# Attention scores of a four-layer block from six bfloat16 products instead of nine, on 64-row halves of TensorE

## The chip, the cores and the metric

The kernel runs on one core of one Trainium2 chip, in one launch. The metric is device time in microseconds (us): 1566.85 us before, the median of three runs (1562.56, 1566.85, 1570.48). The profile shows one further execution with a span of 1563.8 us from its first to its last instruction.

The names of the engines in what follows: PE is TensorE (matmuls), PEld its weight loads, DVE is VectorE, ACT is ScalarE, POOL is GpSimd, SP is SyncE, which here only issues DMAs (SPq in the profile).

## What is computed

An input of 4 sequences of 1024 tokens of 128 features goes through four layers, each added to its input after a normalisation: an RWKV-like time and channel mixing, a mixture of 16 experts, a linear attention with decaying states, and softmax attention followed by a mixture of 8 experts. The change is in the softmax attention of the last layer:

```python
def _gqa(x, wq, wk, wv, wo):                       # 16 heads of 8 features, 4 key heads
    B, S, C = x.shape                              # 4, 1024, 128
    q = (x @ wq.T).reshape(B, S, 16, 8)
    k = (x @ wk.T).reshape(B, S, 4, 8)
    v = (x @ wv.T).reshape(B, S, 4, 8)
    k, v = jnp.repeat(k, 4, axis=2), jnp.repeat(v, 4, axis=2)
    attn = jnp.einsum('bqhd,bkhd->bhqk', q, k) / sqrt(8)
    attn = jnp.where(causal, attn, -inf)
    attn = jax.nn.softmax(attn, axis=-1)
    out = jnp.einsum('bhqk,bkhd->bqhd', attn, v).reshape(B, S, C)
    return out @ wo.T
```

All of it is float32 in the reference. A head has only 8 features, so that a score is a sum over 8 rows of TensorE's 128.

## The kernel before

**The stages.** Up to about 295 us the first layer runs, and the second begins. Up to about 660 us the second layer's experts run beside the linear attention of the first two sequences. From about 660 us on, the softmax attention of all four sequences runs, together with what is left of the linear attention (sequences 2 and 3, generator `stage_c`), the projections `heads`, and the last experts (generator `experts`). This last part stands under `tc.manual_schedule()`: its order is written out by the Python loops and nothing moves it. What stands before it is put into an order by the framework's scheduler.

**Scores from parts.** A float32 matmul of 512 columns keeps PE 0.86 us from start to start in the profile (two instructions), a bfloat16 one 0.22 us. `heads` splits queries and keys into three bfloat16 parts each (`parts3`) and stores them to HBM (`dq`, `dk`, with eight rows d to a part). `spread(b, h)` reads them back for a chunk of 512 tokens, so that nine products (part i of the query with part j of the key) stand under each other as rows of one bfloat16 matmul: 9 products of 8 features are 72 rows (`KROWS`). It issues 18 DMAs on SP, two for each product: one into `keys_r` (L950, 8 rows of 4 key groups), one into `queries_r` (L954, 8 rows of all 16 heads). Rows 125 to 127 (`MROWS` on) hold the row maximum of a query in three parts, against -1 in the keys, so that the score arrives with its maximum subtracted. Rows 72 to 124 are zeros in the queries, set once at the start with memsets on POOL (L868, L869) and two broadcast DMAs for each pair of tiles (L871, L874).

**Two passes over the scores.** For each sequence b and block i of 128 queries:

- `maxima(b, i)` computes scores with the queries as weights and takes row maxima on DVE. `late` treats the keys of the block's own 512-chunk: one matmul a head (L977), as many heads to a PSUM bank as fit (four, two, one, one, for 128, 256, 384, 512 keys), then one matmul of the 128x128 identity with the causal mask `later` that adds -1e30 on the last 128 keys of each head (L981), then a `tensor_reduce` (L985). `early` treats the first 512 keys for blocks 4 to 7, a head at a time: one matmul (L989), one reduce (L990). There are 352 `late` and 256 `early` units in all. Three banks (`to_max`) hold their results. `rows` splits the 16 maxima into three parts on POOL (L999 to L1002); PE turns them (L1005), DVE copies them (L1009), and three DMAs on SP place them into `queries_r` (L1013).
- `weighted(b, i)` computes the scores again with the keys as weights, 128 keys by 4 heads of 128 queries (`unit(j, g)`, L1049, 576 in all; g is one of the 4 key groups, j the key block). ACT takes the exponential (L1054); on the diagonal POOL zeroes what the mask hides (L1058). Two banks (`scores`) hold these. After eight units, four are multiplied with the values (`products`, L1041): four float32 matmuls, each on its own 32 columns of the array, into one bank.

**The order.** The main loop (L1323 to L1347) lets one `unit` of `weighted` run, then as many units of `maxima` of later blocks as the table `COURSE` asks for. Each is a tick; a tick also calls what is due (`later_on`), advances a `spread` by one step (`moving`), and now and then takes a step of `front()` (linear attention and heads of the next sequence) or of `behind_it` (experts of finished chunks). So sc (L1049), sm (L977, L981, L989), av (L1041) and the float32 matmuls of the other stages follow each other on PE in an order that is fixed.

**Weights.** `by_d` (L1397) orders the columns of wq and wk by feature first, so that the rows of `dq` and `dk` come out as `spread` reads them.

Of the kernel before, what the change touches and what calls it, by code (L numbers as in the profile page):

```python
# [12 lines left out]
BF = mybir.dt.bfloat16  # L13
# [5 lines left out]
P = 128  # L19
NB = 4  # L20
T = 1024
CH = 512
NH = T // CH
# [11 lines left out]
def r3(ap, a):  # L35
    return ap.rearrange("p (a b) -> p a b", a=a)
# [3 lines left out]
def sandwich(ctx: ExitStack, tc: tile.TileContext, x, vecs, cmats, rope, wa, wb, wc, wd, out):  # L40
# [3 lines left out]
    nc = tc.nc  # L44
# [718 lines left out]
    while running or behind_a or coming_a:  # L763
        if coming_a and count >= BEHIND:
            b, h = coming_a[0]
# [5 lines left out]
        for item in list(running):  # L771
            kind, b, h, steps = item
# [70 lines left out]
    pk = ctx.enter_context(tc.tile_pool(name="pk", bufs=1, side="left", reuse_waits="tile"))  # L843
    pe = ctx.enter_context(tc.tile_pool(name="pe", bufs=2, side="left", reuse_waits="tile"))
# [3 lines left out]
    nc.sync.dma_start(out=wdt, in_=wd[:, 0:328])  # L848
    identb = pk.tile([P, P], BF, name="identb")
    nc.gpsimd.tensor_copy(identb, ident)  # L850
    later = pk.tile([P, 4, P], BF, name="later")
    m = pe.tile([P, P], FP, tag="a", name="m", bufs=1)
    make_causal_mask(nc, m, MASKED)
    for k in range(4):
        nc.gpsimd.tensor_copy(later[:, k, :], m)
    wv_d, wo_d, wgate_d = wdt[:, 160:192], wdt[:, 192:320], wdt[:, 320:328]
    restart8 = restarts(4, 8, pk, "restart8")
    QSCALE = float(1.0 / np.sqrt(8).astype(np.float32))
# [1 line left out]

    KROWS, MROWS, ROWS = 72, P - 3, P
    keys_r = [pk.tile([P, NH, 4, CH], BF, name=f"keys_r{i}") for i in range(2)]
    queries_r = [pe.tile([P, 16, CH], BF, tag=f"qr{i}", name=f"queries_r{i}", bufs=1) for i in range(NH)]
    for kr, qr in zip(keys_r, queries_r):

        nc.gpsimd.memset(kr[64:128, 0, 0, :], -1.0)  # L868
        nc.gpsimd.memset(qr[64:128, 0, :], 0.0)  # L869
        first, others = qr[64:128, 0:1, :], qr[64:128, 1:16, :]  # L870
        nc.sync.dma_start(out=others, in_=first.to_broadcast([64, 15, CH]))  # L871
        kf = kr.rearrange("p a b t -> p (a b) t")
        first, others = kf[64:128, 0:1, :], kf[64:128, 1 : NH * 4, :]
        nc.sync.dma_start(out=others, in_=first.to_broadcast([64, NH * 4 - 1, CH]))  # L874

    def parts3(dst, src):

# [8 lines left out]
    moved = set()  # L886
# [55 lines left out]
    def spread(b, h):  # L942

        dq, dk = drams[b]
        kr = keys_r[b % 2]
        qr = queries_r[h]
        for i in range(3):
            for j in range(3):
                rows = slice(3 * i + j, KROWS, 9)
                nc.sync.dma_start(  # L950
                    out=kr[rows, h].rearrange("r g t -> r (g t)"),
                    in_=dk[h, j].rearrange("(d g) t -> d (g t)", d=8),
                )
                nc.sync.dma_start(  # L954
                    out=qr[rows].rearrange("r h t -> r (h t)"),
                    in_=dq[h, i].rearrange("(d h) t -> d (h t)", d=8),
                )
                if (i, j) == (2, 2):
                    moved.add((b, h))
                yield  # L960

    def maxima(b, i):


        qr, kr = queries_r[i // 4], keys_r[b % 2]
        tb = slice(i % 4 * P, (i % 4 + 1) * P)
        half = i // 4
        n_s = (i % 4 + 1) * P
        in_bank = CH // n_s
        ms = pe.tile([P, 2, 16], FP, tag="ms", name="ms", bufs=3)  # L970

        def late(h0):
            sc = to_max([P, CH], "sm")
            view = r3(sc[:, : in_bank * n_s], in_bank)
            for k in range(in_bank):
                h = h0 + k
                nc.tensor.matmul(  # L977
                    view[:, k, :], lhsT=qr[0:MROWS, h, tb], rhs=kr[0:MROWS, half, h // 4, 0:n_s],
                    start=(k == 0), stop=False, skip_group_check=True,
                )  # L980
            nc.tensor.matmul(  # L981
                view[:, :, n_s - P :], lhsT=identb, rhs=later[:, :in_bank, :], start=False, stop=True,
                skip_group_check=True,
            )
            nc.vector.tensor_reduce(ms[:, 0, h0 : h0 + in_bank], view, AX.X, ALU.max)  # L985

        def early(h):
            sc = to_max([P, CH], "sm")
            nc.tensor.matmul(sc, lhsT=qr[0:MROWS, h, tb], rhs=kr[0:MROWS, 0, h // 4, :], start=True, stop=True)  # L989
            nc.vector.tensor_reduce(ms[:, 1, h : h + 1], sc, AX.X, ALU.max)  # L990

        def rows():
            mp = pe.tile([P, 3, 16], BF, tag="mp", name="mp", bufs=3)
            left = pe.tile([P, 16], FP, tag="ml", name="ml", bufs=3)
            top = ms[:, 0]
            if half:
                top = pe.tile([P, 16], FP, tag="top", name="top_ms", bufs=3)
                nc.vector.tensor_reduce(top, ms.rearrange("p a h -> p h a"), AX.X, ALU.max)
            nc.gpsimd.tensor_copy(mp[:, 0], top)  # L999
            nc.gpsimd.tensor_sub(left, top, mp[:, 0])  # L1000
            nc.gpsimd.tensor_copy(mp[:, 1], left)
            nc.gpsimd.tensor_sub(mp[:, 2], left, mp[:, 1])  # L1002
            def turned():
                pm = to_max([48, P], "m_ps", BF)
                nc.tensor.transpose(pm, mp.rearrange("p i h -> p (i h)"), identb)  # L1005

                def kept():
                    mt = pe.tile([48, P], BF, tag="mt", name="mt", bufs=3)
                    nc.vector.tensor_copy(mt, pm)  # L1009

                    def placed():
                        for k in range(3):
                            nc.sync.dma_start(  # L1013
                                out=qr[MROWS + k : MROWS + k + 1, :, tb], in_=mt[16 * k : 16 * k + 16, :]
                            )
                        placed_rows.add((b, i))

                    later_on(3, placed)

                later_on(1, kept)  # L1020

            later_on(9, turned)

        units = [lambda h0=h0: late(h0) for h0 in range(0, 16, in_bank)]
        if half:
            units += [lambda h=h: early(h) for h in range(16)]
        return units + [rows]

    def weighted(b, i):


        qr, kr, va = queries_r[i // 4], keys_r[b % 2], vas[b]
        tb = slice(i % 4 * P, (i % 4 + 1) * P)

        def products():

            for _ in range(4):
                j, g, pr = held.popleft()[1:]
                if (j, g) == (0, 0):
                    pavs[b, i] = pp([P, CH], "av")  # L1040
                nc.tensor.matmul(  # L1041
                    pavs[b, i][32 * g : 32 * g + 32, :], lhsT=va[:, j, g, :], rhs=pr, start=(j == 0), stop=(j == i),
                )
            if j == i:
                later_on(1, finish)

        def unit(j, g):
            sc = scores([P, CH], "sc")
            nc.tensor.matmul(  # L1049
                sc, lhsT=kr[0:ROWS, j // 4, g, j % 4 * P : (j % 4 + 1) * P], rhs=qr[0:ROWS, 4 * g : 4 * g + 4, tb],  # L1050
                start=True, stop=True,
            )
            pr = pd.tile([P, CH], FP, tag="pr", name="pr", bufs=10)
            nc.scalar.activation(pr, sc, AF.Exp)  # L1054
            if j == i:

                every = r3(pr, 4)
                nc.gpsimd.affine_select(  # L1058
                    out=every, in_=every, compare_op=ALU.is_ge, fill=0.0, base=0,
                    pattern=[[0, 4], [1, P]], channel_multiplier=-1,  # L1060
                )
            held.append((products, j, g, pr))
            if len(held) > 7:
                held[0][0]()

        def finish():
            av = pd.tile([P, CH], FP, tag="avs", name="av_sb")
            nc.scalar.copy(av, pavs.pop((b, i)))
            if i % 4 == 0:
                sums[b, i // 4] = dram.tile([4, 4, 9, CH], FP, tag="sums", name="sums")  # L1070
            to = sums[b, i // 4].rearrange("g r d t -> g d r t")

            def stored():
                for g in range(4):
                    nc.sync.dma_start(out=to[g][:, :, tb], in_=r3(av[32 * g : 32 * g + 9, :], 4))
                if i % 4 == 3:
# [238 lines left out]
    with tc.manual_schedule():  # L1315
# [7 lines left out]
        for b, i in blocks:  # L1323
# [9 lines left out]
            w = 2 * i * (i + 1)  # L1333
# [36 lines left out]
def _arrays(i):  # L1370
# [25 lines left out]
    wc = [a[L1 + "Wq"], a[L1 + "Wk"], a[L1 + "Wv"], wo_rows, a[L1 + "Wbeta"]]  # L1396
    def by_d(w):  # L1397

        return w.reshape(P, -1, 8).transpose(0, 2, 1).reshape(P, -1)

    wd = [
        by_d(a[F1 + "wq"].T), by_d(a[F1 + "wk"].T), a[F1 + "wv"].T, a[F1 + "wo"].T, a[F1 + "gate_w"].T,
# [24 lines left out]
```

## Time and profile before

| What | Value |
|---|---|
| median of three runs | 1566.85 us |
| profiled execution, span | 1563.8 us |
| DVE busy in it | 1066.1 us |
| ACT busy in it | 845.7 us |
| POOL busy in it | 827.9 us |
| mean granted TensorE clock, as a share of full speed | 0.902 |
| L1049, matmuls sc | 576, 226.1 us busy |
| L977, matmuls sm of `late` | 512, 129.5 us busy |
| L981, mask matmuls of `late` | 352, 88.1 us busy |
| L989, matmuls sm of `early` | 256, 98.1 us busy |
| L1041, matmuls av | 1152 instructions (two for each float32 matmul), 174.9 us busy |
| L1054, exponentials on ACT | 576, 328.2 us busy |
| L985 and L990, maxima on DVE | 608, 213.1 and 166.2 us busy |
| DMAs of `spread` | 72 into `queries_r` of 128 KB, 72 into `keys_r` of 32 KB |
| DMAs that place maxima | 96 of 4 KB |

Matmuls are pipelined: a matmul's own time in the profile includes its way through the array, and the next may start before it ends. So the distance from start to start says what a matmul costs PE, not its duration. The view of chains follows the work back from the last instruction: to what released it, or to the instruction before it on its engine. The view of windows gives the busy time of each engine in a stretch, with the granted clock behind it.

### The profile page before, as it was taken

How to read it: one execution, taken by the hardware profiler on the slowest of the kernel's cores; microseconds unless marked ns; L12 is line 12 of the kernel's file. 1: busy time of each engine (PE TensorE's matmuls, PEld its weight loads, DVE VectorE, ACT ScalarE, POOL GpSimd, SP SyncE). 2: the span in 40 equal slices, each digit the busy share in tenths (PEclk: the TensorE clock that was granted, in tenths of full speed). 3: DMA queues.
4: the chain of work that ended last, by engine and by line, in shares of the span. 5: the costliest groups of instructions: out<-in, count | busy, mean ns of one | idle time of the engine just before them, and what ended most of it. 6: DMA issues, size and time to landing. Idle time of an engine off the chain costs nothing. (4 is left out here: it accounts for less than half of the span.)

```text
span 1563.8 us, 15069 instructions
## 1 busy us (share of the span) xinstructions
PE 1220.8 (78%) x4532; PEld 445.2 (28%) x4532; DVE 1066.1 (68%) x1755; ACT 845.7 (54%) x1565; POOL 827.9 (53%) x901
## 2 busy tenths in 40 slices
PE   4478788868687697877688698779876889889864
PEld 2123333313222232333133223223222333233211
DVE  5886965587757757668976986796379776477501
ACT  3668676536445454545345466534653474655541
POOL 5664575576838857752733655553355554223312
PEclk9779999969888899999889999978897999999986
DMA  3000101452222323101113122211130113111101
GB/s 113 14 7 0 46 29 40 104 117 86 87 60 85 94 68 105 55 19 60 45 53 91 37 58 92 63 53 57 36 98 23 58 43 101 51 55 44 57 24 61
DMA packets 62337, 93.35 MB, mean 60 GB/s; under 512 B 10097, under 2 KB 29809, under 8 KB 61553
## 3 DMA queue, kind: packets, MB, share of 16 engines
q1 hardware_dynamic: 53040, 75.63, 16.8%
q10 hardware_dynamic: 9216, 16.78, 3.3%
q8 instruction: 35, 0.57, 0.2%
q14 instruction: 46, 0.37, 0.1%
HBM read 76.38 MB, written 12.71 MB: 57 GB/s over the span
## 5 line engine op out<-in xcount | busy, mean ns | idle before, releaser
L1054 ACT ACTIVATE pr<-sc 128x512 f32<-128x512 f32 x576 | 328.2, 596 | 298.7 <-PE sc L1049 293.3
L985 DVE TENSOR_REDUCE ms<-sm 128x1 f32<-128x512 f32 (+3 forms) x352 | 213.1, 633 | 120.4 <-PE sm L981 113.7
L1049 PE MATMUL sc<-queries_r,keys_r 128*128 128x512 bf16 x576 | 226.1, 400 | 28.9 <-ACT pr L1054 26.2
L990 DVE TENSOR_REDUCE ms<-sm 128x1 f32<-128x512 f32 x256 | 166.2, 682 | 49.9 <-PE sm L989 49.6
L1041 PE MATMUL av<-pr,va 128*32 128x512 f32 x1152 | 174.9, 660 | 3.7 <-POOL pr L1058 3.7
L1058 POOL TENSOR_SCALAR_AFFINE_SELECT pr<-pr 128x512 f32<-128x512 f32 x128 | 95.2, 758 | 128.8 <-ACT pr L1054 126.8
L977 PE MATMUL sm<-keys_r,queries_r 125*128 125x512 bf16 (+3 forms) x512 | 129.5, 309 | 36.2 <-DVE ms L985 30.5
L1168 POOL TENSOR_TENSOR share<-n,every 128x512 f32<-128x512 f32 x64 | 81.5, 1291 | 84.7 <-DMA every<-row 65.0
L138 PE MATMUL ln_v<-rs,cm 128*128 128x512 f32 x176 | 106.4, 698 | 22.2 <-ACT rs L126 14.7
L989 PE MATMUL sm<-keys_r,queries_r 125*128 125x512 bf16 x256 | 98.1, 405 | 30.4 <-DVE ms L990 25.5
L633 POOL TENSOR_TENSOR kv<-vrep,phi 128x512 f32<-128x512 f32 x64 | 89.0, 1392 | 53.7 <-issue 25.9
L649 POOL TENSOR_TENSOR qs<-st,st 128x512 f32<-128x512 f32 x72 | 102.7, 1428 | 26.5 <-DVE st L639 18.7
L486 POOL TENSOR_TENSOR g<-g,x 128x512 f32<-128x512 f32 x72 | 95.5, 1328 | 30.6 <-ACT g L476 17.9
L478 POOL TENSOR_TENSOR x<-x,gate 128x512 f32<-128x512 f32 x64 | 84.0, 1314 | 36.9 <-ACT g L474 35.7
L1049 PEld LDWEIGHTS <-keys_r 128*128 128x128 bf16 x576 | 57.5, 102 | 137.6 <-issue 111.3
L138 PE MATMUL g_ps<-n,wbt 128*128 128x512 f32 x144 | 81.6, 658 | 18.2 <-DVE n L392 7.5
L465 PE MATMUL y_ps<-g,wbt 128*128 128x512 f32 x144 | 78.3, 629 | 18.1 <-DVE g L496 18.0
L981 PE MATMUL sm<-later,identb 128*128 128x128 bf16 (+2 forms) x352 | 88.1, 250 | 0.0
L138 PE MATMUL u_ps<-n,wbt 128*128 128x512 f32 x144 | 79.4, 634 | 9.8 <-DVE g L496 6.4
L496 DVE TENSOR_TENSOR g<-u_ps,g 128x512 f32<-128x512 f32 x72 | 49.5, 687 | 51.0 <-POOL g L486 31.7
L977 PEld LDWEIGHTS <-queries_r 125*128 125x128 bf16 x512 | 47.6, 100 | 104.1 <-issue 87.6
L1180 PE MATMUL y<-share,wexp 128*128 128x512 f32 x128 | 68.1, 621 | 5.2 <-POOL share L1168 5.0
(302 smaller groups left out, 2311.3 us busy)
## 6 DMA issues: line engine op xcount, KB each, us to landing
gate<-rows ACTq DMA_DIRECT2D x64, 256.0 KB
vrep<-v_rows SPq DMA_DIRECT2D x64, 256.0 KB
every<-row SPq DMA_DIRECT2D x64, 256.0 KB
queries_r<-dq SPq DMA_DIRECT2D x72, 128.0 KB
turn<-in_rope_dram SPq DMA_DIRECT2D x16, 256.0 KB
dq<-qp SPq DMA_DIRECT2D x8, 384.0 KB
keys_r<-dk SPq DMA_DIRECT2D x72, 32.0 KB
sums<-av_sb SPq DMA_DIRECT2D x128, 18.0 KB
```

The source lines that it names most:

```text
L138: nc.tensor.matmul(ps, lhsT=lhsT, rhs=rhs, start=True, stop=True)
L486: nc.gpsimd.tensor_mul(g, g, x)
L633: nc.gpsimd.tensor_mul(kvs[e], values.pop(e), k)
L649: nc.gpsimd.tensor_add(sums_e[e][0], s0, s1)
L977: nc.tensor.matmul(view[:, k, :], lhsT=qr[0:MROWS, h, tb], rhs=kr[0:MROWS, half, h // 4, 0:n_s], start=(k == 0), stop=False, skip_group_ch ...
L985: nc.vector.tensor_reduce(ms[:, 0, h0 : h0 + in_bank], view, AX.X, ALU.max)
L989: nc.tensor.matmul(sc, lhsT=qr[0:MROWS, h, tb], rhs=kr[0:MROWS, 0, h // 4, :], start=True, stop=True)
L990: nc.vector.tensor_reduce(ms[:, 1, h : h + 1], sc, AX.X, ALU.max)
L1041: nc.tensor.matmul(pavs[b, i][32 * g : 32 * g + 32, :], lhsT=va[:, j, g, :], rhs=pr, start=(j == 0), stop=(j == i),)
L1049: nc.tensor.matmul(sc, lhsT=kr[0:ROWS, j // 4, g, j % 4 * P : (j % 4 + 1) * P], rhs=qr[0:ROWS, 4 * g : 4 * g + 4, tb], start=True, stop=True,)
L1054: nc.scalar.activation(pr, sc, AF.Exp)
L1058: nc.gpsimd.affine_select(out=every, in_=every, compare_op=ALU.is_ge, fill=0.0, base=0, pattern=[[0, 4], [1, P]], channel_multiplier=-1,)
```

## The change

Six products are kept of nine: parts (0,0), (0,1), (1,0), (1,1), (0,2) and (2,0). With 8 features these are 48 rows, and three rows for the maximum make 51, which fit into 64. So two sets of rows lie in one tile: partitions 0 to 63 hold key groups 0 and 2 and heads 0 to 7 as the tiles count them, partitions 64 to 127 the other eight heads. `by_d` reorders the weights, so that the d-rows of a part come as 16 rows, for the two halves. In each half, row 8d+n holds product n of feature d; the maxima lie in slot 6 of features 0 to 2, and slot 7 is zero in the queries.

- `late`, `early` and `unit` read 64 partitions, of the one or the other half. Units take the halves in turn: g % 2 in `weighted`, n in `maxima`. The program puts these matmuls on 64x128 tiles of the array, at row 0 or row 64.
- The mask's identity would need 128 rows, so it is split: keys 0 to 63 of a block (`upper`, 128 columns a head) and keys 64 to 127 (`lower`, 64 columns a head), two matmuls of 64 rows for each `late` unit. Both are kept in both halves (`id_part`, `upper`, `lower`: 20 copies on POOL instead of 4).
- The maxima's rows are read in `maxima` too now, so that they must be zero by then: `spread` of the sequences after the first begins with a DMA that copies slot 7 onto slot 6.
- `spread` issues 12 DMAs (13 with that copy) in place of 18, of 16 partitions each, in 6 steps in place of 9; the placing of maxima 2 in place of 3, of 24 rows of 128 each.
- The tiles `keys_r` and `queries_r` are half as large. They are filled at the start by memsets of 128 partitions, and by eight broadcast DMAs into slots 6 and 7 alone, in place of four into 64 partitions.

```diff
-    later = pk.tile([P, 4, P], BF, name="later")
     m = pe.tile([P, P], FP, tag="a", name="m", bufs=1)
     make_causal_mask(nc, m, MASKED)
-    for k in range(4):
-        nc.gpsimd.tensor_copy(later[:, k, :], m)
+    HALF = P // 2
+    id_part = pk.tile([P, 2, P], BF, name="id_part")
+    upper = pk.tile([P, 4, P], BF, name="upper")
+    lower = pk.tile([P, 4, HALF], BF, name="lower")
+    for to in (slice(0, HALF), slice(HALF, P)):
+        for n in range(2):
+            nc.gpsimd.tensor_copy(id_part[to, n, :], identb[n * HALF : (n + 1) * HALF, :])
+        for k in range(4):
+            nc.gpsimd.tensor_copy(upper[to, k, :], m[0:HALF, :])
+            nc.gpsimd.tensor_copy(lower[to, k, :], m[HALF:P, HALF:])
...
-    KROWS, MROWS, ROWS = 72, P - 3, P
-    keys_r = [pk.tile([P, NH, 4, CH], BF, name=f"keys_r{i}") for i in range(2)]
-    queries_r = [pe.tile([P, 16, CH], BF, tag=f"qr{i}", name=f"queries_r{i}", bufs=1) for i in range(NH)]
...
+    PAIRS = [(0, 0), (0, 1), (1, 0), (1, 1), (0, 2), (2, 0)]
+    SLOTS, TOP = 8, 6
+    keys_r = [pk.tile([P, NH, 2, CH], BF, name=f"keys_r{i}") for i in range(2)]
+    queries_r = [pe.tile([P, 8, CH], BF, tag=f"qr{i}", name=f"queries_r{i}", bufs=1) for i in range(NH)]
+    for t, val in [(kr.rearrange("p a b t -> p (a b) t"), -1.0) for kr in keys_r] + [(qr, 0.0) for qr in queries_r]:
+
+        n = t.shape[1]
+        nc.gpsimd.memset(t[:, 0, :], val)
+        for slot in (TOP, TOP + 1):
+            first, others = t[slot::SLOTS, 0:1, :], t[slot::SLOTS, 1:n, :]
+            nc.sync.dma_start(out=others, in_=first.to_broadcast([P // SLOTS, n - 1, CH]))
...
@@ spread
-        for i in range(3):
-            for j in range(3):
-                rows = slice(3 * i + j, KROWS, 9)
...
+        if b:
+            nc.sync.dma_start(out=qr[TOP::SLOTS], in_=qr[TOP + 1 :: SLOTS])
+        for n, (i, j) in enumerate(PAIRS):
+            rows = slice(n, P, SLOTS)
+            nc.sync.dma_start(
+                out=kr[rows, h].rearrange("r g t -> r (g t)"),
+                in_=dk[h, j].rearrange("(d g) t -> d (g t)", g=2),
+            )
+            nc.sync.dma_start(
+                out=qr[rows].rearrange("r h t -> r (h t)"),
+                in_=dq[h, i].rearrange("(d h) t -> d (h t)", h=8),
+            )
...
@@ maxima
         def late(h0):
+            rows, first = half_of(h0 // 8), h0 % 8
...
-                    view[:, k, :], lhsT=qr[0:MROWS, h, tb], rhs=kr[0:MROWS, half, h // 4, 0:n_s],
+                    view[:, k, :], lhsT=qr[rows, h, tb], rhs=kr[rows, half, h // 4, 0:n_s],
...
-                view[:, :, n_s - P :], lhsT=identb, rhs=later[:, :in_bank, :], start=False, stop=True,
+                view[:, :, n_s - P :], lhsT=id_part[rows, 0, :], rhs=upper[rows, :in_bank, :], start=False, stop=False,
+                skip_group_check=True,
+            )
+            nc.tensor.matmul(
+                view[:, :, n_s - HALF :], lhsT=id_part[rows, 1, :], rhs=lower[rows, :in_bank, :], start=False, stop=True,
...
-            nc.tensor.matmul(sc, lhsT=qr[0:MROWS, h, tb], rhs=kr[0:MROWS, 0, h // 4, :], start=True, stop=True)
+            nc.tensor.matmul(
+                sc, lhsT=qr[rows, h % 8, tb], rhs=kr[rows, 0, h % 8 // 4, :], start=True, stop=True
+            )
...
-                        for k in range(3):
+                        for n in range(2):
+                            first = n * HALF + TOP
                             nc.sync.dma_start(
-                                out=qr[MROWS + k : MROWS + k + 1, :, tb], in_=mt[16 * k : 16 * k + 16, :]
+                                out=qr[first : first + 3 * SLOTS : SLOTS, :, tb], in_=mt[24 * n : 24 * n + 24, :]
                             )
...
-        units = [lambda h0=h0: late(h0) for h0 in range(0, 16, in_bank)]
+        units = [lambda h=h0 + 8 * n: late(h) for h0 in range(0, 8, in_bank) for n in range(2)]
         if half:
-            units += [lambda h=h: early(h) for h in range(16)]
+            units += [lambda h=h + 8 * n: early(h) for h in range(8) for n in range(2)]
...
@@ weighted
+            rows, of = half_of(g % 2), g // 2
...
-                sc, lhsT=kr[0:ROWS, j // 4, g, j % 4 * P : (j % 4 + 1) * P], rhs=qr[0:ROWS, 4 * g : 4 * g + 4, tb],
+                sc, lhsT=kr[rows, j // 4, of, j % 4 * P : (j % 4 + 1) * P], rhs=qr[rows, 4 * of : 4 * of + 4, tb],
...
@@ by_d
-        return w.reshape(P, -1, 8).transpose(0, 2, 1).reshape(P, -1)
+        return w.reshape(P, 2, 2, -1, 8).transpose(0, 2, 4, 1, 3).reshape(P, -1)
```

More of the change, by code (lines that the diff above doesn't have):

```diff
@@ L858, in sandwich, with half_of @@
     QSCALE = float(1.0 / np.sqrt(8).astype(np.float32))
-    KROWS, MROWS, ROWS = 72, P - 3, P
-    keys_r = [pk.tile([P, NH, 4, CH], BF, name=f"keys_r{i}") for i in range(2)]
-    queries_r = [pe.tile([P, 16, CH], BF, tag=f"qr{i}", name=f"queries_r{i}", bufs=1) for i in range(NH)]
[L866 to L874, printed above, removed]
+    PAIRS = [(0, 0), (0, 1), (1, 0), (1, 1), (0, 2), (2, 0)]
[8 more added lines that the diff above has]
+            nc.sync.dma_start(out=others, in_=first.to_broadcast([P // SLOTS, n - 1, CH]))
+    def half_of(half):
+        return slice(half * HALF, (half + 1) * HALF)
     def parts3(dst, src):
@@ L946, in spread @@
         qr = queries_r[h]
-        for i in range(3):
-            for j in range(3):
-                rows = slice(3 * i + j, KROWS, 9)
[L950 to L960, printed above, removed]
+        if b:
[10 more added lines that the diff above has]
+            )
+            if n + 1 == len(PAIRS):
+                moved.add((b, h))
+            yield
     def maxima(b, i):
@@ L975, in late @@
             for k in range(in_bank):
-                h = h0 + k
+                h = first + k
                 nc.tensor.matmul(
-                    view[:, k, :], lhsT=qr[0:MROWS, h, tb], rhs=kr[0:MROWS, half, h // 4, 0:n_s],
+                    view[:, k, :], lhsT=qr[rows, h, tb], rhs=kr[rows, half, h // 4, 0:n_s],
                     start=(k == 0), stop=False, skip_group_check=True,
@@ L987, in early @@
         def early(h):
+            rows = half_of(h // 8)
             sc = to_max([P, CH], "sm")
-            nc.tensor.matmul(sc, lhsT=qr[0:MROWS, h, tb], rhs=kr[0:MROWS, 0, h // 4, :], start=True, stop=True)
+            nc.tensor.matmul(
+                sc, lhsT=qr[rows, h % 8, tb], rhs=kr[rows, 0, h % 8 // 4, :], start=True, stop=True
+            )
             nc.vector.tensor_reduce(ms[:, 1, h : h + 1], sc, AX.X, ALU.max)
         def rows():
-            mp = pe.tile([P, 3, 16], BF, tag="mp", name="mp", bufs=3)
+            mp = pe.tile([P, 2, 3, 8], BF, tag="mp", name="mp", bufs=3)
             left = pe.tile([P, 16], FP, tag="ml", name="ml", bufs=3)
@@ L998, in rows @@
                 nc.vector.tensor_reduce(top, ms.rearrange("p a h -> p h a"), AX.X, ALU.max)
[L999 to L1002, printed above, removed]
+            top, left = r3(top, 2), r3(left, 2)
+            nc.gpsimd.tensor_copy(mp[:, :, 0], top)
+            nc.gpsimd.tensor_sub(left, top, mp[:, :, 0])
+            nc.gpsimd.tensor_copy(mp[:, :, 1], left)
+            nc.gpsimd.tensor_sub(mp[:, :, 2], left, mp[:, :, 1])
             def turned():
                 pm = to_max([48, P], "m_ps", BF)
-                nc.tensor.transpose(pm, mp.rearrange("p i h -> p (i h)"), identb)
+                nc.tensor.transpose(pm, mp.rearrange("p a i h -> p (a i h)"), identb)
                 def kept():
```

## The prediction

> **What bounds the kernel now.** I read the page first: busy shares, then the chain that ended last.
>
> ```profile
> PE 1220.8 (78%) x4532; PEld 445.2 (28%) x4532; DVE 1066.1 (68%) x1755; ACT 845.7 (54%) x1565; POOL 827.9 (53%) x901
> PE 19%; DVE 7%; ACT 4%; POOL 2%; issue 2%; SPq 2%; DMA 2%; POOLq 0%; ACTq 0%; DVEq 0%
> ```
>
> The chain covers 38% of the span only, its last 600 us; there PE holds half of it (19 of 38). The change lives in the stage from 660 us on, so I looked at that by windows of 50 us (busy time of PE, PEld, DVE, ACT, POOL, granted clock, DMA share, GB/s):
>
> ```profile
> 1000.00:1050.00 50.00, 33.27 (x142) 10.47 (x140) 46.75 (x59) 20.24 (x48) 32.36 (x26) 0.83 0.20 61
> 1150.00:1200.00 50.00, 33.62 (x153) 10.79 (x151) 44.05 (x60) 22.08 (x40) 28.88 (x25) 0.89 0.27 79
> 1300.00:1350.00 50.00, 47.06 (x262) 17.64 (x261) 25.91 (x47) 29.36 (x53) 16.82 (x29) 0.99 0.20 61
> 1450.00:1500.00 50.00, 43.43 (x217) 13.54 (x216) 17.29 (x44) 31.63 (x59) 14.53 (x19) 1.00 0.14 46
> ```
>
> Two regimes: where linear attention runs beside, DVE is full and PE has slack (33 of 50); where it doesn't, PE is full (47 of 50) and DVE and ACT are half idle. So what the change does to PE's own column of work counts for about half. The queue of exponentials confirms who is late: ACT waits 293.3 us for sc (L1049) in all.
>
> Then PE's timeline, start to start, in a full stretch:
>
> ```profile
> 1301.55 0.38 PE L989 MATMUL sm<-keys_r,queries_r 125*128 125x512 bf16 x1
> 1301.77 0.38 PE L1049 MATMUL sc<-queries_r,keys_r 128*128 128x512 bf16 x1
> 1302.08 1.07 PE L1041 MATMUL av<-pr,va 128*32 128x512 f32 x8
> 1303.08 0.39 PE L989 MATMUL sm<-keys_r,queries_r 125*128 125x512 bf16 x1
> ...
> 1308.87 1.02 PE L1180 MATMUL y<-share,wexp 128*128 128x512 f32 x2
> 1309.73 0.38 PE L1049 MATMUL sc<-queries_r,keys_r 128*128 128x512 bf16 x1
> ...
> 1359.33 0.22 PE L981 MATMUL sm<-later,identb 128*128 128x128 bf16 x1
> 1359.39 0.38 PE L1049 MATMUL sc<-queries_r,keys_r 128*128 128x512 bf16 x1
> ```
>
> Three prices come from it. A bfloat16 matmul of 512 columns costs 0.22 us (1301.55 to 1301.77), a mask of 128 columns 0.06. Going to the 32-column tiles of av costs 0.09 (sc to av is 0.31, not 0.22). Eight av instructions take 1.00 us where two instructions of that length on the full array take 0.86 (y to sc): four tiles of columns run side by side, and the way back costs some 0.10, once 0.04 for their staggered starts are off. Between float32 and bfloat16 on the full array nothing is lost (the 0.86).
>
> **The change, part by part.** I compared the two programs' instruction order: from the first score on, PE's matmuls follow each other as before, but for the added masks. The parts then:
>
> 1. Changes of tiling. Scores leave the full array for 64-row tiles, the float32 matmuls between them stay. Counted in the order: 377 changes of tile shape before, 679 after, so 302 more, each way between scores and float32. No row shows a change of rows; the nearest are the changes of columns, 0.09 and 0.10. In the timeline 263 of these 302 neighbours follow back to back, without a wait that could hide it. 263 x 0.10 = +26 us. Bounds: nothing, if rows change free of charge, to 302 x 0.10 = +30. I take +26.
>
> 2. Masks. 352 more matmuls, of 64 columns for each head in the bank: 256 units with one head, 64 with two, 32 with four. 128 columns cost 0.06, 256 cost 0.11 (read the same way), 64 between half of 0.06 and all of it, for each brings a weight load. 256 x 0.045 + 64 x 0.06 + 32 x 0.11 = +19 us; bounds 15 and 23.
>
> 3. Two halves at once. A matmul can run beside the one before it if that uses the other half. Counted: 340 such pairs with a long first matmul (85 sc to late, 61 sc to early, 95 early to sc, 55 sc to sc, 44 early to early). In 171 further ones the first is only the new short mask, worth nothing. By the waits of before, some 290 of the 340 are back to back; in the rest the second waits for ACT or DVE. The most a pair can save is its 0.22 less a start step of 0.01, as av's column tiles do: 290 x 0.21 = 61 us; the least is nothing. Between them lies the weight load:
>
> ```profile
> 1442.24 0.38 PE L977 MATMUL sm<-keys_r,queries_r 125*128 125x512 bf16 x1
> 1442.24 0.10 PEld L981 LDWEIGHTS <-identb 128*128 128x128 bf16 x1
> ```
>
> The next weights load when the matmul before starts, for 0.10 us. If so here too, the second starts 0.10 later and a pair saves 0.12 of its 0.22: 290 x 0.115 = -33 us. I take that, as nearest to how loads are issued now. A late unit gains little even so: where its half is that of the sc before it, it is longer by one mask.
>
> PE's sum: 26 + 19 - 33 = +12 us; from -46 (15 - 61) to +53 (30 + 23). On the path counts half: +6, from -23 to +27.
>
> [...]
>
> 4. DMAs. In `spread` SP issues at 0.65 us each, and what stands behind waits:
>
> ```profile
> 1144.10 0.67 SPq L950 DMA_DIRECT2D keys_r<-dk x1
> 1144.87 0.65 SPq L954 DMA_DIRECT2D queries_r<-dq x1
> ...
> 1158.94 1.90 SPq L629 DMA_DIRECT2D vrep<-v_rows x3
> ```
>
> 18 x 0.65 = 11.7 us become 13 x 0.65 = 8.5, so -3.2. The chain has such a row of issues at two places (1144 and 1354 us), where linear attention's vrep and the experts' den stand behind: -6 us together; bounds 0 (the next wait is there already) and -10 (one more spread counts). The other spreads are hidden behind PE and DVE. The added copy of slot 7 is among the 13; it waits for the same readers as the DMA that was first before. Placing maxima saves one issue of some 0.58 us for each of 32 blocks, off the path, for sc waited 1.9 us on it in all; its new waits on PE are for maxima that are older than the transposition it waits for anyway.
>
> 5. The start. POOL's 4 mask copies at 0.29 and 4 memsets at 0.52 become 20 copies and 4 memsets, some 16 x 0.29 = +4.6 us at 295 us, where DVE waits 4.5 us for POOL (g, L486). Against that the fill moves 0.6 MB in place of 2.8, where DMA is busy 0.92 and 0.49 of two windows of 10 us. And the scheduler orders the stage of 300 to 660 us slightly otherwise. Between -8 and +8, taken as 0.
>
> 6. ACT, DVE and POOL do the same reads and writes per unit: 0.
>
> Sum: +6 - 6 + 0 = 0 against the span of 1563.8. The median of runs stands 3 us above that, so 1567 us. Its own range goes about half way to the bounds of parts 1 to 5, -15 and +18: 1552 to 1585.
>
> **The rivals.**
>
> A, faster: the halves truly overlap at 0.01 us and a change of rows is free. PE -46, on the path half, -23, with the DMAs' -6 and up to -5 at the start: 1567 - 32 = 1535. For it: av's tiles overlap almost wholly, and ACT and DVE have room in full stretches. Against: DVE binds elsewhere, and changes of columns do cost.
>
> B, slower: the halves do not overlap, because each score's weights follow the matmul before it in one queue. Then parts 1 and 2 stand alone: +45 on PE, up to 53. It decides once pairs save under some 0.06 us, half of what I take. Where PE is full most of it shows: 0.6 x 45 = +27, less 6: 1588. For it: no row here shows two matmuls on different rows side by side. Against: the column tiles.
>
> C, slower still: the granted clock drops, because half the array idles in a score or PE has more gaps. The rows have 0.83 where PE is busy 33 of 50 us, 0.99 at 47 of 50, so less work on PE goes with a lower clock. From 0.93 (the mean of the windows of 650 to 1500 us) to 0.83 PE's 704 us busy in them grow by 12%, +84, half on the path: 1567 + 42 = 1609. Against: in full stretches there is a margin.
>
> **How the numbers follow.** Forecast, about no change: 0.38. A 0.25, B 0.25, C 0.12. 0.5%, about 8 us, is what a measurement of this kernel can tell from no change. Within the forecast I put 0.09 below 1559, 0.20 within, 0.09 above 1575; A gives 0.23 faster and 0.02 same, B 0.23 slower and 0.02 same, C 0.12 slower. Faster 0.32, same 0.24, slower 0.44. The range reaches to A's and beyond B's time, 1538 to 1605, leaving out some 0.1 at each end.
>
> **What would show it.** Part 1: start to start from y to sc grows from 0.86 to some 0.95. Part 3: sm to sc on other halves starts 0.10 apart (A: 0.01, B: 0.22). Part 2: the second mask to the next score some 0.05. Part 4: 13 issues in a spread, vrep 3 us sooner behind them. C: the clock below 0.9 in windows with PE above 40 of 50. I am wrong if PE's column moves as said but DVE's or ACT's waits, not PE, take or give the time; or if the stage before 660 us moves by more than 8 us.

## The result and the profile after

The changed kernel takes 1589.77 us, median of four runs (1588.77 to 1593.25), beside 1568.66 us for the kernel before on the same chip (four runs, 1562.56 to 1572.84). The ratio of the runs is 1.0148, 95% interval 1.0118 to 1.0178; by the medians the kernel is 21 us slower. The profiled span is 1587.2 us (1563.8 before).

The page of the kernel after, busy shares and then the chain that ended last:

```profile
PE 1234.2 (78%) x4884; PEld 414.5 (26%) x4884; DVE 1066.7 (67%) x1755; ACT 843.6 (53%) x1565; POOL 826.5 (52%) x917
...
PE 19%; DVE 7%; ACT 4%; POOL 2%; issue 2%; DMA 1%; SPq 0%; POOLq 0%; ACTq 0%; DVEq 0%
```

DVE, ACT and POOL do the same work to within 2.1 us each. On the chain the queue of SP went from 2% to 0%: there the removed DMA issues show. PE has 352 more instructions, the masks, and only 13 us more busy time. So far nothing says where 23 us went. The windows do (busy time of PE, PEld, DVE, ACT, POOL, granted clock, DMA share, GB/s):

```profile
750.00:800.00 50.00, 34.30 (x150) 8.53 (x150) 45.70 (x56) 18.83 (x44) 32.51 (x27) 0.69 0.13 39
900.00:950.00 50.00, 40.66 (x242) 12.06 (x235) 43.00 (x58) 27.75 (x51) 26.75 (x32) 0.84 0.14 39
1000.00:1050.00 50.00, 36.06 (x168) 9.91 (x161) 39.99 (x58) 23.43 (x52) 22.39 (x20) 0.76 0.20 60
1150.00:1200.00 50.00, 38.80 (x205) 11.45 (x204) 37.71 (x51) 28.10 (x51) 25.65 (x31) 0.87 0.27 80
1200.00:1250.00 50.00, 39.61 (x161) 11.69 (x161) 46.72 (x75) 18.24 (x33) 32.33 (x27) 0.69 0.15 45
1300.00:1350.00 50.00, 45.45 (x271) 15.59 (x263) 33.32 (x75) 26.39 (x50) 24.34 (x35) 0.93 0.25 78
1450.00:1500.00 50.00, 41.95 (x236) 11.88 (x234) 33.75 (x73) 28.68 (x53) 11.63 (x18) 0.93 0.16 51
```

In the four windows that were shown of before, the clock goes from 0.83, 0.89, 0.99, 1.00 to 0.76, 0.87, 0.93, 0.93, though PE is about as busy. In the stage of the scores, 660 to 1510 us, the same view gives 0.93 before and 0.86 after for the whole.

Now PE's timeline, to be read from start to start (start, duration, then the instruction; a number in brackets is idle time before it):

```profile
1319.12 1.93 PE L1061 MATMUL av<-pr,va 128*32 128x512 f32 x8
1320.98 0.60 PE L1005 MATMUL sm<-keys_r,queries_r 64*128 64x512 bf16 x1
...
1326.84 1.06 PE L1061 MATMUL av<-pr,va 128*32 128x512 f32 x8
1327.83 1.13 PE L1184 MATMUL y<-n,cm 128*128 128x512 f32 x2
1328.89 0.39 PE L1005 MATMUL sm<-keys_r,queries_r 64*128 64x512 bf16 x1
1328.90 0.39 PE L1070 MATMUL sc<-queries_r,keys_r 64*128 64x512 bf16 x1
...
1335.50 0.22 PE L996 MATMUL sm<-lower,id_part 64*128 64x128 bf16 x1
1335.56 0.38 PE L1070 MATMUL sc<-queries_r,keys_r 64*128 64x512 bf16 x1
...
1342.10 0.38 PE L1070 MATMUL sc<-queries_r,keys_r 64*128 64x512 bf16 x1
1342.40 1.12 PE L1201 MATMUL y<-share,wexp 128*128 128x512 f32 x2
1343.46 0.28 PE L988 MATMUL sm<-keys_r,queries_r 64*128 64x256 bf16 x1
```

- Two products on different halves start 0.01 us apart (1328.89 and 1328.90), where 0.22 was needed before. The halves overlap whole.
- A float32 pair between scores is dearer: from sc into it 0.30 (1342.10 to 1342.40, before 0.22), and 1.06 until the next product (1327.83 to 1328.89 and 1342.40 to 1343.46, before 0.86). Among the trace's pairs at the full clock, 128 follow a tile of another shape; in nearly all of them the second of the two instructions starts 533 ns after the first, and not 428. The next score or mask product starts 525 ns after the second, and not 428. Together with the way in that is some 0.29 us a pair.
- The first two lines lie in a stretch at the half clock: eight av instructions take 1.86 us until the next start, not the 0.99 of 1326.84.

The queue of SP in a `spread` (start, duration, the DMA):

```profile
1165.10 0.57 SPq L957 DMA_DIRECT2D queries_r<-queries_r x1
...
1174.08 3.75 SPq L1096 DMA_DIRECT2D sums<-av_sb x8
1177.88 1.83 SPq L629 DMA_DIRECT2D vrep<-v_rows x3
```

Its 13 issues take 9.0 us (1165.10 to 1174.08), where 18 took 11.9 before (1144.10 to 1155.95).

**One account for all runs.** Three terms make up the stretch from the first `sm` to the last `sc`: time in which no matmul runs on PE; the time in which one runs, counted as if the clock had been full; and what the half clock adds to it. In this trace the granted clock is either 1.0 or 0.5 (54 records of each), so the last term is half of the busy time that lies in stretches at 0.5. I worked this out from the matmul records of each trace, overlaps counted once, in us:

| Kernel | stretch | PE idle | work at full clock | added by half clock |
|---|---|---|---|---|
| before | 849.3 | 147.1 | 650.2 | 52.0 |
| after | 872.9 | 160.1 | 612.6 | 100.3 |
| after less before | +23.6 | +13.0 | -37.6 | +48.3 |

PE has less to do than before, and the lower clock takes back more than that. Each row rests on one execution, and the executions of one kernel differ by 3 to 15 us. A caution on the split: it takes everything at the half clock to last twice as long. What does not scale (a wait between two tiles, perhaps) belongs to the work, which then falls by less; I come back to how much. The sum of the two, +10.7, does not depend on it.

### The profile page after: what moved, and what is told of

It reads as the page before. It is cut to its first block, busy times and chain, and to the rows that moved or that the text cites. A ratio compares the mean times of both kernels' runs of the same rounds, so it can differ in the third digit from the quotient of the medians.

```text
span 1587.2 us, 15708 instructions
## 1 busy us (share of the span) xinstructions
PE 1234.2 (78%) x4884; PEld 414.5 (26%) x4884; DVE 1066.7 (67%) x1755; ACT 843.6 (53%) x1565; POOL 826.5 (52%) x917
## 5 line engine op out<-in xcount | busy, mean ns | idle before, releaser
L1070 PE MATMUL sc<-queries_r,keys_r 64*128 64x512 bf16 x576 | 211.6, 423 | 40.0 <-ACT pr L1075 38.4
L1061 PE MATMUL av<-pr,va 128*32 128x512 f32 x1152 | 186.3, 708 | 0.6 <-POOL pr L1079 0.5
L988 PE MATMUL sm<-keys_r,queries_r 64*128 64x512 bf16 (+3 forms) x512 | 117.5, 323 | 29.5 <-DVE ms L1000 26.3
L138 PE MATMUL ln_v<-rs,cm 128*128 128x512 f32 x176 | 110.8, 724 | 24.7 <-ACT rs L126 14.7
L1005 PE MATMUL sm<-keys_r,queries_r 64*128 64x512 bf16 x256 | 91.5, 437 | 40.1 <-DVE ms L1008 30.8
L1070 PEld LDWEIGHTS <-keys_r 64*128 64x128 bf16 x576 | 48.2, 97 | 166.5 <-issue 160.8
L496 DVE TENSOR_TENSOR g<-u_ps,g 128x512 f32<-128x512 f32 x72 | 49.5, 687 | 53.2 <-POOL g L486 33.1
L992 PE MATMUL sm<-upper,id_part 64*128 64x128 bf16 (+2 forms) x352 | 79.3, 257 | 0.0
L1201 PE MATMUL y<-share,wexp 128*128 128x512 f32 x128 | 72.2, 652 | 5.7 <-POOL share L1189 5.4
L474 ACT ACTIVATE g<-x 128x512 f32<-128x512 f32 x72 | 44.6, 622 | 42.1 <-DVE x L472 42.0
```

What stands on the lines that cost most here:

```text
L138: nc.tensor.matmul(ps, lhsT=lhsT, rhs=rhs, start=True, stop=True)
L988: nc.tensor.matmul(view[:, k, :], lhsT=qr[rows, h, tb], rhs=kr[rows, half, h // 4, 0:n_s], start=(k == 0), stop=False, skip_group_check=True,)
L1005: nc.tensor.matmul(sc, lhsT=qr[rows, h % 8, tb], rhs=kr[rows, 0, h % 8 // 4, :], start=True, stop=True)
L1061: nc.tensor.matmul(pavs[b, i][32 * g : 32 * g + 32, :], lhsT=va[:, j, g, :], rhs=pr, start=(j == 0), stop=(j == i),)
L1070: nc.tensor.matmul(sc, lhsT=kr[rows, j // 4, of, j % 4 * P : (j % 4 + 1) * P], rhs=qr[rows, 4 * of : 4 * of + 4, tb], start=True, stop=True,)
L1201: nc.tensor.matmul(y, lhsT=wexp[:, e, :], rhs=shares[e], start=False, stop=(e == 7))
```

## The experiments

Theory R: the granted clock follows the rows of TensorE that are at work, so a product on 64 rows counts half, and the clock that this loses is the time lost. Theory L: the time follows a ledger of PE's work, changes of tile shape and masks against overlap, and the clock only goes along. Times are medians; the kernel before stands at 1568 to 1569 in all these comparisons.

**Six products without the halves.** The number of products alone, on the full array:

```
-    KROWS, MROWS, ROWS = 72, P - 3, P
+    PAIRS = [(0, 0), (0, 1), (1, 0), (1, 1), (0, 2), (2, 0)]
+    KROWS, MROWS, ROWS = 48, P - 3, P
...
+        for n, (i, j) in enumerate(PAIRS):
+            rows = slice(n, KROWS, 6)
```

> Six products of 48 rows, but on the full array as before (zero rows to 124, maxima at 125 to 127, one mask matmul). Theory R (the granted clock goes by rows at work, so that a 64-row matmul counts half): PE's work and rows are as before, the clock of the scores' stage stays at 0.93 +- 0.01, and only the DMAs count: 1558 to 1568 us. Theory L (the ledger of tile changes and masks against overlap; the clock only follows from how full PE is): the same time, for none of the three is here. A clock below 0.90 would speak against both.

Measured: 1560.92, ratio 0.9952 (0.9934 to 0.9971). This version is 7.2 us, 0.5%, faster than the kernel before. PE's work is the same to 1.1 us (649.1 for 650.2) and its idle time is 6.6 us less (140.5 for 147.1), so the gain is that of the shorter spread. The halves and their masks then cost 1589.77 - 1560.92 = 29 us. The stretch of this kernel is the base of most that follows (beside linear attention and after it; busy PE, PEld, DVE, ACT, POOL, clock):

```profile
660.00:1100.00 440.00, 353.40 (x1668) 128.07 (x1667) 346.25 (x563) 224.11 (x433) 213.73 (x240) 0.92 0.18 54
1100.00:1510.00 410.00, 352.39 (x1764) 123.94 (x1762) 252.56 (x470) 239.44 (x436) 166.77 (x216) 0.95 0.17 51
```

**All heads on one half.** The changed kernel, but with every head's rows on rows 0 to 63, so that nothing can overlap; tiles of 64 rows and the masks in two parts stay:

```
-    keys_r = [pk.tile([P, NH, 2, CH], BF, name=f"keys_r{i}") for i in range(2)]
+    keys_r = [pk.tile([P, NH, 4, CH], BF, name=f"keys_r{i}") for i in range(2)]
...
-            rows, of = half_of(g % 2), g // 2
...
-                sc, lhsT=kr[rows, j // 4, of, j % 4 * P : (j % 4 + 1) * P], rhs=qr[rows, 4 * of : 4 * of + 4, tb],
+                sc, lhsT=kr[0:ROWS, j // 4, g, j % 4 * P : (j % 4 + 1) * P], rhs=qr[0:ROWS, 4 * g : 4 * g + 4, tb],
```

> All 16 heads on rows 0 to 63: tile changes and both masks as in the changed kernel, but no two matmuls can overlap. R: rows at work are counted as in the changed kernel while each score holds PE longer, so the clock of the scores' stage stays at 0.86 or below and the time goes above the changed kernel's: 1600 to 1630 us. L: PE is fuller than before the change (+45 us), so the clock is 0.93 or above, and the time 1588 to 1600 us.

Measured: 1676.38, ratio 1.0691 (1.0646 to 1.0736), far above both.

```profile
660.00:1100.00 440.00, 398.81 (x1633) 129.86 (x1634) 312.47 (x496) 200.91 (x387) 195.53 (x219) 0.73 0.16 48
1100.00:1510.00 410.00, 373.92 (x1629) 119.90 (x1621) 234.39 (x432) 196.02 (x356) 151.88 (x194) 0.78 0.17 49
```

The second is the line to read twice. PE is busy 374 of 410 us, more than the 352 above, and yet the clock is 0.78 and not 0.95. So it isn't gaps on PE that lower it; the narrow products do. In the account the half clock adds 205.6 us here. Changes of shape and masks are here too, but the next two experiments leave them out as causes: they hardly move the clock. That the clock goes with the rows is shown; that it is only a follower (L) falls. The time it costs was larger than either theory had it.

**The changes of shape by themselves.** Six products on all rows, but each score and mask split into two products of 64 weight columns, side by side; this makes 627 changes of tile shape rather than 377, without halving the rows at work:

```
+                for c in (0, 64):
+                    nc.tensor.matmul(
+                        sc[c : c + 64, :], lhsT=kr[0:ROWS, j // 4, g, j % 4 * P + c : j % 4 * P + c + 64],
+                        rhs=qr[0:ROWS, 4 * g : 4 * g + 4, tb], start=True, stop=True,
+                    )
```

> The six products on the full array's rows, but every score and mask matmul split into two of 64 weight columns, on the two column halves side by side: 627 changes of tile shape in place of 377 (the changed kernel has 679), all 128 rows at work, one mask. R: the clock stays at 0.93, the changes of shape cost 250 x 0.1 = 25 us of PE, a third to a half on the path: 1566 to 1575 us, so that most of the 28 us between the first run and the changed kernel is the clock. L: changes of shape are the cost: 1575 to 1590 us at a clock of 0.93.

Measured: 1599.16, ratio 1.0186 (1.0144 to 1.0228): 38 us above the six products, more than either theory had.

```profile
660.00:1100.00 440.00, 357.98 (x2375) 129.94 (x2377) 335.97 (x544) 214.46 (x415) 202.62 (x224) 0.91 0.17 52
1100.00:1510.00 410.00, 360.04 (x2574) 133.67 (x2567) 262.80 (x487) 226.07 (x409) 166.21 (x219) 0.95 0.17 51
```

The clock is that of the base, 0.91 and 0.95 for 0.92 and 0.95, so it is out of this; in the account the half clock adds 0.5 us, the work grows by 42.3 and idle time falls by 3.7. And the timeline of this kernel has the prices of the changed one:

```profile
1343.90 0.38 PE L986 MATMUL sm<-later,identb 128*64 128x512 bf16 x2
1344.22 1.13 PE L1190 MATMUL y<-share,wexp 128*128 128x512 f32 x2
1345.27 0.41 PE L1059 MATMUL sc<-queries_r,keys_r 128*64 128x512 bf16 x2
```

Into the float32 pair 0.32, out of it 1.05. In the trace 163 such runs of float32 leave back to back to a product (94 ns more each), 111 are entered back to back (some 90 ns), and in up to 137 the second instruction is late by 105 ns: 15.3 + 10.0 + 14.4 = 40 us. The time rose by 38. Nearly all of it is on the path.

**The masks.** Twice: the changed kernel without `lower` (keys 64 to 127 of the diagonal block are left unmasked in the maxima), and the full-array kernel with 352 masks more that add zero.

```
-            nc.tensor.matmul(
-                view[:, :, n_s - HALF :], lhsT=id_part[rows, 1, :], rhs=lower[rows, :in_bank, :], start=False, stop=True,
-                skip_group_check=True,
-            )
```

> The changed kernel without its second mask matmul (lower): keys 64 to 127 of the diagonal block are left unmasked in the maxima for all queries. R: the short masks cost a few us and the clock stays where it is: 1582 to 1590 us. L: 352 x 0.05 = 18 us of PE go, half on the path: 1577 to 1583 us.

```
+            nc.tensor.matmul(
+                view[:, :, n_s - P // 2 :], lhsT=identb, rhs=nothing[:, :in_bank, :], start=False, stop=True,
+                skip_group_check=True,
+            )
```

> The six products on the full array (the first of these runs, 1561 us) with a second mask matmul of 64 columns a head that adds zeros, for each of the 352 late units. PE's column grows by 352 x 0.05 = 18 us at full rows. The forecast's part 2 (half on the path): 1568 to 1572 us. By the run without the lower mask, which gave nothing: 1559 to 1565 us, for what it costs in full stretches it gives back in rows at work.

Measured: 1590.66 without (1.0148, 1.0121 to 1.0174; the changed kernel has the same ratio), 1565.29 with the added ones, 4.4 us above the base. In the account the masks are 10.7 us of work in the changed kernel (612.6 less 601.9) and 13.3 on the full array (662.4 less 649.1). But without them the half clock adds 8.3 us more and PE is idle 3.4 more; with them on the full array it adds 4.2 less, idle time is 4.5 less. Work that is taken from PE is not time, as long as the clock and the idle time take its place.

**More work for PE.** The maxima products of one head are issued twice for the first two sequences (256 more), in the changed kernel and on the full array. This is the edit in `early`; the loop of `late` is doubled likewise for 384 and 512 keys:

```
+            for _ in range(2 if b < 2 else 1):
+                nc.tensor.matmul(
+                    sc, lhsT=qr[rows, h % 8, tb], rhs=kr[rows, 0, h % 8 // 4, :], start=True, stop=True
+                )
```

> The changed kernel with the 512-column matmuls of early and the 384- and 512-column ones of late issued twice in sequences 0 and 1 (256 more matmuls; the second overwrites the first with the same sums). R: the clock of 660 to 1130 us rises from 0.81 to 0.87 or more, and this pays for most of the work: 1583 to 1596 us. L: 256 x 0.215 = 55 us more on PE, partly overlapped, half on the path: 1600 to 1618 us, whatever the clock.

> The six products on the full array with the same 256 matmuls issued twice in sequences 0 and 1 as were doubled in the changed kernel, where they cost 12 us (and the clock rose from 0.81 to 0.87). R: here the clock is high already (0.92 to about 0.95 in 660 to 1100 us), so the work is less paid for: 15 to 30 us more than 1561, 1576 to 1591. L: the clock has no part in it, and the cost is the same 12 us or less: 1565 to 1574.

Measured: 1601.68 (1.0214, 1.0173 to 1.0256), 11.9 us above the changed kernel, where L's bracket is just met and R's is missed; and 1577.59 (1.0057, 1.0038 to 1.0075), 16.7 above its base, where R's is just met and L's is missed. The extra work raised the clock from 0.81 to 0.87 between 660 and 1100 us in the changed kernel, as R says, but on the full array it rose as well, from 0.92 to 0.95. In the account the work grows by 38.8 us in the changed kernel and by 45.8 on the full array; the half clock gives back 8.9 and 10.1 of it, idle time 18.0 and 17.2. So the 5 us between the two costs are not the clock's, and a clock that comes back pays for about a quarter of the work that brings it.

**Fewer changes of shape.** The float32 steps that are owed beside the attention are taken up only in the tick after av products, so that they stand in longer rows: 565 changes, not 679. The control is the same on the full array (368, not 377).

```
+            after_av[0] = True
...
-        if owed[0] >= 1.0:
+        grouped = after_av[0]
+        after_av[0] = False
+        while owed[0] >= (1.0 if grouped else MOST):
```

> The changed kernel, with the owed float32 steps beside the attention (linear attention's and the output projection's) taken up only in the tick that follows av products, several at once, so that float32 products stand in longer rows and the tile shape changes 565 times rather than 679. The same edit on the six products of the full array (the control, run beside it) takes only 9 changes away. L (each change of shape has a price, 0.15 us by the run with scores split in columns: 38 us for 250): 114 fewer changes are worth about 17 us, so that the distance of this kernel to its control shrinks from 29 us (1589.8 to 1560.9) to 10 to 16. R (the 29 us are mainly the clock that half the rows cost): the distance stays at 24 to 32, because the rows at work are the same. The grouping itself may delay maxima or av products; this shows in the control as well and drops out of the distance.

> The control of the grouped order: six products of 48 rows a head on the full array, masks as before, owed float32 steps taken up only in the tick that follows av products. 368 changes of tile shape rather than 377, so both theories, R and L, expect 1556 to 1575 (1560.9 without the grouping): what it differs by is what the grouping itself costs in delays.

Measured: 1607.89 (1.0245, 1.0203 to 1.0286) and 1572.73 (1.0029, 1.0005 to 1.0053). The grouping itself costs 11.8 us: in both, what follows the last score takes about 17 us longer, for steps are left over until then. The distance is 35 us, so L's 10 to 16 are out, and R's 24 to 32 are just passed. The account tells why. In us, against the full-array kernel of the same order:

| Pair | stretch | PE idle | work at full clock | added by half clock |
|---|---|---|---|---|
| after less six products | +32.5 | +19.6 | -36.5 | +49.5 |
| grouped less its control | +37.9 | +27.7 | -53.0 | +63.3 |

The 114 changes did save their 16.5 us of work, what L had expected (17). They were lost again to the clock (13.8 more) and to idle time (8.1 more).

```profile
660.00:1100.00 440.00, 334.83 (x1735) 106.14 (x1730) 336.52 (x531) 209.00 (x409) 202.89 (x224) 0.83 0.16 49
```

That is the grouped kernel; its control:

```profile
660.00:1100.00 440.00, 343.55 (x1660) 126.69 (x1664) 349.81 (x566) 222.50 (x433) 209.56 (x241) 0.91 0.17 50
```

**Less overlap.** Only the order of units is changed, so that fewer neighbours lie on different halves (340 long ones to 236); rows, masks and changes of shape stay. The control takes the same order of scores on the full array.

```
-        units = [lambda h=h0 + 8 * n: late(h) for h0 in range(0, 8, in_bank) for n in range(2)]
+        units = [lambda h=h0 + 8 * n: late(h) for n in range(2) for h0 in range(0, 8, in_bank)]
...
-        return [lambda j=j, g=g: unit(j, g) for j in range(i + 1) for g in range(4)]
+        return [lambda j=j, g=g: unit(j, g) for j in range(i + 1) for g in (0, 2, 1, 3)]
```

> The changed kernel with the order of its units altered so that fewer neighbours lie on different halves: maxima go through the heads of the one half first and then of the other, scores take the key groups as 0, 2, 1, 3. The same matmuls, the same rows and the same 679 changes of tile shape; neighbours on different halves with a long first matmul fall from 340 to 236. By the order of the instructions (a matmul may start once its own half is free and the one before has started; a column at the shortest pitch of the trace, 0.42 ns) running side by side can save 70 us of PE's time in the changed kernel and 41 in this one. L (the time is PE's ledger, and what runs side by side counts in full): the 29 us come back as 1610 to 1622. R (the clock, which goes by the rows at work, takes back a good part of what the overlap gives; less overlap also means PE is busier in a window only in time, not in rows): 1594 to 1608.

> The control of the altered order: six products of 48 rows a head on the full array with scores in the order of key groups 0, 2, 1, 3 (maxima go through the heads in turn there anyway). Nothing overlaps, nothing is added: both theories expect the 1560.9 without the altered order, 1555 to 1567. What it differs by is the price of the order itself.

Measured: 1624.84 (1.0373, 1.0330 to 1.0416) and 1565.31 (0.9983, 0.9966 to 1.0000). Less the control's 4.4, the lost overlap costs 30.7 us, about the 29 that the order of the instructions gave, as L said (its bracket is passed by 3 us, which the price of the order explains); R's bracket is missed. But the clock moved here. The changed kernel first, then the altered order:

```profile
660.00:1100.00 440.00, 350.19 (x1762) 108.04 (x1761) 336.86 (x548) 212.66 (x415) 202.51 (x228) 0.81 0.17 52
1100.00:1510.00 410.00, 344.88 (x1925) 107.68 (x1923) 259.94 (x483) 229.56 (x420) 173.30 (x223) 0.91 0.18 53
...
660.00:1100.00 440.00, 362.11 (x1710) 117.45 (x1712) 331.26 (x536) 207.84 (x405) 201.57 (x223) 0.80 0.17 51
1100.00:1510.00 410.00, 359.31 (x1838) 117.78 (x1842) 253.18 (x457) 217.03 (x393) 161.49 (x212) 0.86 0.17 49
```

In the account the work rises by 27.4 us, the half clock adds 31.7 more and PE is idle 22.2 less. So the time agrees with the lost overlap as a sum, in which more half clock and less idle time nearly cancel.

So neither theory stands alone. The changes of shape are paid nearly in full on PE, as L has it, and the overlap is a gain in PE's work as L counts it; the clock is a second bill of the same size, set by the rows at work, as R has it.

## Why the prediction came out as it did

The forecast was about no change, 1567 us; 1590 is 23 above it, within the range and outside the forecast's own 1552 to 1585. That it lies within the range is in part luck, and that rival B's 1588 is nearest is luck altogether, for B's halves don't overlap. The sum of the forecast held the overlap at about half its size, some 30 us too small, and the half clock at nothing, where the account has 48 us; these two errors cancelled in part. What made the kernel slower is in the main rival C's clock, with dearer changes of shape; it came together with the full overlap of rival A, which none of the cases had combined.

- **Part 1, changes of tiling: mis-sized.** +26 us were taken from 0.10 for each of 263 changes. The same kind of change measured by itself cost 38 us for 250, 0.15 each, because three prices meet in a float32 pair: 0.09 on the way in, 0.10 on the way out, and 0.105 between its two instructions. The last was not in the pairs that the forecast read, where the two stood 428 ns apart. But the kernel before has 533 too, in the 25 pairs at the full clock that follow av or the turned maxima, another tile shape each. Here 0.96 us pass from y to the next product, not 0.86:

```profile
1306.37 1.12 PE L1163 MATMUL y<-n,cm 128*128 128x512 f32 x2
1307.33 0.38 PE L989 MATMUL sm<-keys_r,queries_r 125*128 125x512 bf16 x1
```

So this term could have been read before the change. That a weight load is what stands between the two is only argued.

- **Part 2, masks: too large.** +19 as work; 11 to 13 measured, and 0 to 4 in time.
- **Part 3, overlap: the wrong end chosen.** The step that failed is "if so here too, the second starts 0.10 later". The second starts 0.01 later; the weight load, 0.09 us from 1328.89 on for the product at 1328.90, doesn't hold it up. That is the 61 us end of the bounds, or 70 with short products counted (by the order of instructions), not 33; in the account the kernel on one half has 59.9 us more work than the changed one. In this trace 287 products start within 100 ns after a long one on 64 rows, 193 of them 3 to 10 ns after it.
- **Half on the path: failed, to both sides.** The changes of shape counted nearly in full, 38 us of time for 42 of work (columns), and the clock did not move. The doubled maxima counted for about a third, 16.7 us for 45.8 on the full array, and the added masks too, 4.4 for 13.3; there the half clock and idle time gave the rest back. The lost overlap cost 30.7 us for 27 of work, but with a lower clock and less idle time in the sum. So no single share holds. The windows with a full DVE did not shield the changes of shape; such windows are averages, and PE waits and works in turn within them.
- **Part 4, DMAs: right.** -6 was forecast, -7.2 measured by the six products on the full array.
- **Part 5, the start: nearly right.** The first `sm` starts at 660.5 us, 0.1 us later than before. The first `sc` starts some 4 us later, at 686.7; but the six products on the full array have 687.8, so this isn't the halves' doing.
- **Rival B** fell (the halves do overlap). **Rival A**'s overlap came, its free changes did not. **Rival C** had the clock fall "because half the array idles in a score or PE has more gaps": the first is shown by the kernel on one half, where PE has fewer gaps. Its sign came, a clock of 0.84 with PE at 40.66 of 50 us (900 to 950). Its 0.83 was 0.86, and its +84 on PE was 48 by the account.

How these make the +32.5 us of the stretch over the six products: the terms of PE's work measured alone are 40 for changes, 11 for masks and up to -70 for overlap, -19 in all; with 19.6 of idle time that leaves some 32 for the half clock. The account has -36.5 and 49.5 for the same two. The same test on the kernel on one half, where nothing overlaps, has 40 + 11 = 51 of work against 23.4 in the account (672.5 - 649.1). So the split between work and clock remains uncertain by about 18 us in the changed kernel, and by 28 where the half clock holds longer; by both, clock and idle time took more than the overlap, less its costs, gave. Why PE is idle 13 us more than before was not tried by itself; in the runs idle time moves against PE's busy time (22 less idle with 59 us more busy in the run with less overlap), as it must where other engines set part of the pace.

What would help was found too: the fewer products alone, 1560.92 us, 7 us faster than the kernel before.

## What to carry to other kernels

Before packing narrow matmuls side by side, weigh two bills: each float32 pair between the packed products cost about 0.29 us more in this stream, and rows left idle counted as idle time for the clock here, so that a well-filled PE was still slowed (on one half, busy for 374 of 410 us at a clock of 0.78). Make an account of idle time, work at full clock and time added by the half clock before and after a change; a busy share hides all three. Try the parts of a change alone: here the plain one, fewer products and DMAs, was the whole gain.

## What was not expected of the hardware

- A product on 64 rows counted about half for the clock here. In the traces of before and after the clock changes in steps of 3.41 us: all its records but the last, 89 and 107, are whole numbers of such steps long. For each step between 660 and 1510 us I summed PE's work: each product for the time in which its columns stream, a product on 64 rows as half of it, together at most the whole step. A column stands for 0.42 ns at the full clock (512 in bfloat16 start 0.215 us apart at the closest in the kernel before), for twice that in float32 (0.428 us for 512), and for double the time at the half clock. From the full clock, the half clock followed in the next step exactly when that share was below a bound just under 0.38: before, the 24 steps with a fall have at most 0.361 and the other 189 at least 0.380; after, the 29 with a fall have at most 0.379 and the other 149 at least 0.383. With that bound 6 of the 178 steps after are falsely told when such a product counts 0.4, 4 when it counts 0.6, and 11 by time alone, where the best bound, 0.465, still leaves 6. The way back to full is told less sharply: with a bound of 0.74, 1 step of 35 is false before and 6 of 70 after. Gaps have their part still: of the 29 falls to the half clock after the change, time alone would tell 18 (before, all 24); the other 11 come with the halved rows.
- A change of tile shape also costs time inside the float32 pair that follows it. The runs have a price on either side of such a change, 0.09 us in and 0.10 out; beside these, the second instruction of the pair starts 533 ns after the first, and not 428.
